# First ffn of an eight-phase model on one core: one product for router and latent, expert weights with the first stage, another pace of the sort

## The chip, the cores and the metric

The kernel runs on one core of one Trainium2 chip. The metric is the device time of one execution in microseconds (us), the median of the runs shown. All data are 32-bit floats unless a line says otherwise. The engines are named as in the profile: PE is TensorE's matrix product, PEld its weight load, DVE VectorE, ACT ScalarE, POOL GpSimd, SP SyncE, which here only issues DMAs.

## The reference

The input x is 8 batches of 256 tokens of 256 numbers. Eight sub-layers run one after the other, and after each comes x = layernorm(x + sublayer(x)): attention and feed-forward (ffn) in turn, four of each. The change touches the end of the first attention (attn0), the first ffn (ffn0), and in small ways the start of the second attention (attn1) and the last ffn's sort. attn0 is causal attention with 16 heads of 16 over 4 key heads. ffn0 is

```
scores = sigmoid(x @ gate.T)                  # 32 experts in 4 groups of 8
sb     = scores + gate_bias
groups = the 2 groups with the largest sum of their top two sb
chosen = top 8 of sb within the two groups
wts    = scores at chosen, over their sum, times 2.5
lat    = x @ fc1.T                            # 256 -> 128
routed = sum over chosen of wts_e * (relu(lat @ w1_e.T)**2 @ w2_e.T)
out    = routed @ fc2.T + relu(x @ shared_up.T)**2 @ shared_down.T
```

w1 and w2 are 32 matrices of 128 x 128 each, 2 MB each.

## The kernel before

The rows of x stay in SBUF for the whole kernel, as X[b] (tokens on partitions) and, transposed, as xT, four blocks of 512 tokens (two batches). A phase is a function; its weights are loaded on SP's queue by a `_load` function while the phase ahead runs, into a pool that lies at the other end of SBUF than the pool of the running phase. Working tiles of a phase are in a pool `act`, closed at its end. PSUM has four tags, "t", "a", "s" and "o", of two banks each. In attn0, ffn0, attn1, ffn2, attn3 and ffn3 the compute engines run in the order in which the code names the operations; work is interleaved by Python generators, where each `yield` hands over to another strand.

**attn0** (line 241). The loop over eight batches (480 to 512) runs, for batch b, the maxima of batch b+1, the exponentials of b, and between them `fill`, which takes one step of `finish` of an earlier batch, sometimes one step of a strand `ahead` (projections, at the end ffn0's shared expert on block 0), and two steps of the strand `sorting`. `finish` (386 to 439) makes the values, transposes them, multiplies by wo, adds and normalizes, and in its next step calls `norm_done(b)`, which transposes X[b] into xT (line 145). Behind batch 3 that step also starts the sort of ffn0's token group 0 (batches 0 to 3), so that it runs beside batches 4 to 7. `spread` (346) transposes HL, which POOL makes.

**The sort of a token group** (`ffn0_sort`, 947, with `place`, 840, `tile_experts`, 908, and `scatter`, 922). Each group has 8 tiles of 128 tokens. The sort computes the logits (962), sigmoid, the latents (977, copied twice by ACT, since each token goes to two expert groups), the two groups of each token, where each token's row comes to lie (counts and ranks, two products at 871), which expert group each tile belongs to (`r_te`, transposed at 917), and the weights of the eight experts. Then 16 indirect DMAs from POOL (928) write rows of 128 latents and 8 weights (544 bytes each) to a buffer `lrows` in DRAM, sorted by expert group.

**The experts** (`ffn0_experts`, 1071). Each token group gives 19 tiles of sorted rows, each of one expert group. SP fetches two tiles at a time as `xg` (1083). A tile is transposed (1099), multiplied by eight matrices of w1 (1107, two half steps), put through relu by ACT (1112) and squared by POOL (`hg`, 1114), multiplied by w2 (1124), and summed with its weights by DVE (1133, 1135); the sum goes to DRAM (`louts`, 1137). 19 tiles are 40 steps. `ffn0_combine` (1150 and on) gathers each token's two rows back, adds them, multiplies by fc2 and normalizes.

**ffn0** (1193) puts the strands in order: both expert weights are loaded into its `act` pool, each in four DMAs, on SP's queue behind attn1's weights (three of 2 MB). Then the shared expert on block 1 (`ffn0_shared`, 1042: four products up, each with relu and square, then two down), with the rest of attn0's strand and the first steps of group 1's sort; then group 0's 19 tiles beside group 1's sort; then the shared expert on blocks 2 and 3 beside `combine(0)`; then group 1's tiles beside the rest of it; `combine(1)` goes on into attn1.

**attn1** (1243) projects keys, queries and values per batch and group of heads (1273).

The shape of ffn0's order before is:

```
for i, _ in enumerate(self.ffn0_shared(w, 1, act)):
    if i == 1:
        for x in left:
            for _ in x:
                pass
    if i >= 2:
        next(sort, None)
    if i == 3:
        next(tiles)
for _ in tiles:
    next(sort, None)
```

Of the kernel before, what the change touches and what calls it, by code (L numbers as in the profile page):

```python
# [18 lines left out]
P = 128  # L19
# [20 lines left out]
class Model:  # L40
# [199 lines left out]

    def attn0(self, w, act, start=False, beside_then=None, between=()):

# [115 lines left out]
        def weights(b):  # L358

            qT, kT, o = qTs[b // 2], kTs[b // 2], (b % 2) * T  # L360
            for i, (kc, qc) in enumerate(((0, 0), (0, 1), (1, 1))):
# [15 lines left out]
                for s in range(4):  # L377
                    p = act.tile([P, 4, P], F32, tag=f"pT{i}{s}", name="pT")
                    nc.scalar.activation(p.rearrange("p h q -> p (h q)"), ps[s], AF.Exp)
                    if kc == qc:  # L380
                        nc.gpsimd.affine_select(
                            p, p, pattern=[[0, 4], [1, P]], compare_op=ALU.is_ge, fill=0.0,
                            base=0, channel_multiplier=-1,
                        )
                    pT[b, i, s] = p
                yield

        def finish(b):
# [48 lines left out]
            yield  # L437
            self.norm_done(b)
            if beside_then and b == GROUPS0[0][1] - 1:
                sorting.append(beside_then(act))  # L440
            yield

# [13 lines left out]

        ends, ahead, sorting, calls = [], [], [], [0]

# [6 lines left out]
        def fill(every=2):  # L465
            step(ends)
            calls[0] += 1
            if calls[0] % every == 0:
                step(ahead)
            for _ in range(2):  # L470
                step(sorting)

        def drain():
            while ahead:
                step(ahead)

        for _ in project(0):
            pass
# [3 lines left out]
        for b in range(NB):  # L482
            nxt = None
            if b == 0 or b % 2 == 1:
                drain()
                if (b + 3) // 2 < NBLK:
                    ahead.append(project((b + 3) // 2))
            if b + 1 < NB:
                nxt = maxima(b + 1)
            else:  # L490
                ahead.append(between)
            next(prev, None)
            mine = weights(b)
            for i in range(3):
                if nxt is not None:
                    next(nxt)
                fill(2 if b else 1)
                if i == 0:
                    spread(b)
                next(mine)  # L500
                fill(2 if 0 < b < NB - 1 else 1)
            if b == NB - 1:
                while ends:
                    step(ends)
            ends.append(finish(b))
            prev = nxt

        for _ in range(5):
            fill(1)
        while ahead or sorting:  # L510
            fill(1)
        return ends

# [331 lines left out]
    def place(self, w, act, keep, name, idx, n, E=32, tag="t"):  # L845
# [17 lines left out]
        )  # L863
        yield

        count, rank = (
# [41 lines left out]
    def tile_experts(self, w, act, keep, name, ends, tag="t"):  # L908

        nc, E = self.nc, ends.shape[1]  # L910
        past = act.tile([P, E], F32, tag="r_past", name="r_past", bufs=1)
        nc.vector.tensor_scalar(past, ends, w["iota"][:, 32:33], None, ALU.is_le)
        te = act.tile([P, 1], F32, tag="r_te", name="r_te", bufs=1)
        nc.vector.tensor_reduce(te, past, AX.X, ALU.add)
        nc.vector.tensor_scalar(te, te, float(E - 1), None, ALU.min)
        pt = self.ps(tag)[0:1, :P]
        nc.tensor.transpose(pt, te, self.ident)
# [19 lines left out]
    def ffn0_load(self, pool, keep):  # L937
        return dict(
            gate=self.load(pool, "f0_gate", [P, 2, 32]),
            bias=self.load_row(pool, "f0_bias", 32),  # L940
            fc1=self.load(pool, "f0_fc1", [P, 2, P]),
            behind=self.load(pool, "c_behind", [P, P]),
# [6 lines left out]
    def ffn0_sort(self, w, g, act, keep, tag="a"):  # L949
# [8 lines left out]

        lg = self.ps(tag)[:, : n * 32].rearrange("p (t e) -> p t e", e=32)
        for t in range(n):  # L960
            for c in range(2):
                nc.tensor.matmul(
                    lg[:, t, :], x(t, c), w["gate"][:, c, :], start=(c == 0), stop=(c == 1)
                )
        sc = act.tile([P, n, 32], F32, tag="r_sc", name="r_sc", bufs=1)
        nc.scalar.activation(sc, lg, AF.Sigmoid)
        sb = act.tile([P, n, 32], F32, tag="r_sb", name="r_sb", bufs=1)
        nc.vector.tensor_tensor(
            sb, sc, w["bias"].unsqueeze(1).to_broadcast([P, n, 32]), ALU.add
        )  # L970
        yield
        lat = keep.tile([P, n, 2, ROW0], F32, tag="lat", name="lat", bufs=1)
        for i in range(0, n, 4):
            pl = self.ps(tag).rearrange("p (t l) -> p t l", t=4)
            for t in range(4):
                for c in range(2):
                    nc.tensor.matmul(
                        pl[:, t, :], x(i + t, c), w["fc1"][:, c, :], start=(c == 0), stop=(c == 1)
                    )
            for k in range(2):  # L980
                nc.scalar.copy(lat[:, i : i + 4, k, 0:P], pl)
            yield

# [27 lines left out]
        )  # L1011
        expert = self.tile_experts(w, act, keep, f"f0{g}", ends, tag=tag)
        yield
# [25 lines left out]
        self.sorted0[g] = slots, expert  # L1039
        yield from self.scatter(self.lrows[g], slots, lambda t, k: lat[:, t, k, :])  # L1040

# [150 lines left out]

    def ffn0(self, w, act, keep, left, start=False):

# [3 lines left out]

        w1, w2 = (
            self.load(act, x, [P, 32, P], split=4).rearrange("p (g e) f -> p g (e f)", g=4)  # L1200
            for x in ("f0_w1", "f0_w2")
        )
        if 0 not in self.sorted0:
            if start:
                for b in range(NB):
                    self.transpose_x(b)
            for _ in self.ffn0_sort(w, 0, act, keep):
                pass
            for _ in self.ffn0_shared(w, 0, act):
                pass  # L1210
        sort = self.ffn0_sort(w, 1, act, keep)
        tiles = self.ffn0_experts(w1, w2, 0, act)
        for i, _ in enumerate(self.ffn0_shared(w, 1, act)):
            if i == 1:
                for x in left:
                    for _ in x:
                        pass
            if i >= 2:
                next(sort, None)
            if i == 3:  # L1220
                next(tiles)
        for _ in tiles:
# [4 lines left out]
        tiles = self.ffn0_experts(w1, w2, 1, act)  # L1227
        for blk in range(2, 4):
            for i, _ in enumerate(self.ffn0_shared(w, blk, act)):
                next(put, None)  # L1230
                if blk == 3 and i == 3:
                    next(tiles)
        for _ in tiles:
# [12 lines left out]
    def attn1(self, w, act, beside, then, start=False):  # L1246
# [6 lines left out]
        w["wo"] = self.load(act, "a1_wo", [P, 16, D], split=2)  # L1253
        gqk = act.tile([P, 1], F32, tag="gqk", name="gqk", bufs=1)
        nc.vector.tensor_tensor(gqk, w["gq"], w["gk"], ALU.mult)
        attTs, ends = {}, []

        class Unit:
# [5 lines left out]
            def begin(u):  # L1264
                u.qT = act.tile([P, 4, T], F32, tag="qT", name="qT")
                u.kT = act.tile([P, 4, T], F32, tag="kT", name="kT")
                u.rq = self.small.tile([P, 8], F32, tag="rq", name="rq")
                u.ssq = self.small.tile([P, 8], F32, tag="ssq", name="ssq")

            def project(u, which, t):  # L1270
                ps = self.ps("a")
                for c in range(2):
# [11 lines left out]
            def keys(u, t):  # L1284
                ps = u.kps[t] = u.project("wk", t)
                ssk = self.small.tile([P, 4], F32, tag="ssk", name="ssk")
# [28 lines left out]
            def turned(u, x, t):  # L1315
# [3 lines left out]
                tok = slice(t * P, (t + 1) * P)  # L1319
                if x is u.q:  # L1320
                    nc.vector.tensor_copy(u.qT[:, :, tok], pt)
                else:
                    nc.scalar.mul(u.kT[:, :, tok], pt, gqk)
# [537 lines left out]
    def ffn3_sort(self, w, g, act):  # L1861
# [33 lines left out]
        next(rows)  # L1895
        expert = self.tile_experts(w, act, self.const, f"f3{g}", ends)

# [157 lines left out]
def tile_layers(ctx: ExitStack, tc: tile.TileContext, ins, out, phases):  # L2055
# [6 lines left out]
    def open_weights(i):  # L2062
# [3 lines left out]
        if phases[i] in ("ffn0", "attn3"):  # L2066
# [3 lines left out]
            )  # L2070
            args = [kept[i]]
        pool = s.enter_context(tc.tile_pool(name=f"w{i}", bufs=1, side=sides[i % 2]))
        stack[i] = (s, load(pool, *args))
# [3 lines left out]
    for i, name in enumerate(phases):  # L2077
        m.last = i == len(phases) - 1
        with tc.tile_pool(name=f"act{i}", bufs=2, side=sides[i % 2]) as act:
# [3 lines left out]
            with tc.manual_schedule(engines=COMPUTE) if name in MANUAL else ExitStack():  # L2083
                if name == "attn0":
                    beside = None
                    if not m.last:
                        beside = partial(m.ffn0_sort, stack[i + 1][1], 0, keep=kept[i + 1])
                    between = iter(())
                    if not m.last:
                        between = m.ffn0_shared(stack[i + 1][1], 0, act, ("qT", "kh0"), bufs=3)  # L2090
                    left = m.attn0(w, act, start, beside, between)
                elif name == "ffn0":
                    left = m.ffn0(w, act, kept[i], left, start=start)
                elif name == "attn1":
# [19 lines left out]
def lay_out(i):  # L2114
# [24 lines left out]
    o["a0_wo"] = tiles(L0["attn_wo"])  # L2139
    o["f0_gate"] = tiles(L0["ffn_gate_w"].T)  # L2140
    o["f0_bias"] = L0["ffn_gate_bias"][None]
    o["f0_fc1"] = tiles(L0["ffn_fc1_w"].T)
    o["f0_fc2"] = L0["ffn_fc2_w"].T
# [94 lines left out]
```

## Time and profile before

| | |
|---|---|
| Median of 3 runs | 2625.83 us (2614.57 to 2627.1) |
| Profiled execution | 2678.61 us, its span 2676.9 us, mean granted TensorE clock 0.923 |
| Data moved by DMA in the span | 120.75 MB, 45 GB/s on average |
| Stretch of attn0 and ffn0 | from the start to about 580 us |
| First product of an expert | 361.30 us |
| Last steps of group 0's tiles | about 460 us |

The profile page shows one execution, in the span of which every instruction has a start and an end. Its second part cuts the span into 40 slices of 67 us and gives each engine's busy share in tenths, with the clock that TensorE was granted (`PEclk`, in tenths of full speed). A list of waits gives, for one engine, the instruction that stood idle (line and destination), what ended the wait, and the total, number and longest of such waits in us. A timeline row gives start, duration, engine, line, operation and operands, and in brackets the idle time before it with its releaser; on SP's queue a row is the issue of DMAs, and "x8" stands for eight of them. A table of windows gives, for a stretch, its length, the busy time (and number of instructions) of PE, PEld, DVE, ACT and POOL, the granted clock, the busy share of the 16 DMA engines and GB/s. A 32-bit product counts as several matmul records.

### The profile page before, as it was taken

The numbers are of one execution on the slowest core, as the hardware profiler recorded it, in microseconds if no ns is written. First come the engines' busy times: TensorE is split into PE (matmuls) and PEld (weight loads), VectorE is DVE, ScalarE is ACT, GpSimd is POOL, SyncE is SP. The second block draws the span as 40 slices with busy tenths as digits, with TensorE's granted clock in tenths as the row PEclk, the third lists the DMA queues.
The fourth block names the chain that finished last, engine by engine and source line by source line (L and its number), as shares of the span: only waits on it lengthen the run. The fifth ranks groups of instructions, "written<-read, shape, count | busy, mean of one in ns | idle before, by whom it ended". The sixth has DMA issues, their size and how long they took to land. (4 is left out here: it accounts for less than half of the span.)

```text
span 2676.9 us, 36134 instructions
## 1 busy us (share of the span) xinstructions
PE 2261.8 (84%) x12024; PEld 1535.6 (57%) x12080; DVE 1455.2 (54%) x3645; ACT 1020.2 (38%) x2911; POOL 934.1 (35%) x1637
## 2 busy tenths in 40 slices
PE   8997768989999999999999999997877777676780
PEld 4454457765666666666664465555555544465570
DVE  3546347665454444445455444556988887442353
ACT  1222224335454444445432112222767656433340
POOL 1221326444343333233312321001666648422315
PEclk9987879999999999999999999999989987687895
DMA  4000221110000100000070011002000001334553
GB/s 119 1 1 4 108 80 52 28 51 4 4 5 3 49 1 1 1 1 1 9 253 1 0 48 48 1 0 96 1 1 1 1 7 42 105 128 136 158 158 96
DMA packets 92451, 120.75 MB, mean 45 GB/s; under 512 B 9901, under 2 KB 79726, under 8 KB 91246
## 3 DMA queue, kind: packets, MB, share of 16 engines
q1 hardware_dynamic: 82846, 96.15, 11.1%
q0 software_dynamic: 8192, 21.11, 2.5%
q8 instruction: 101, 1.65, 0.2%
q10 hardware_dynamic: 1232, 1.18, 0.1%
q14 instruction: 80, 0.66, 0.1%
HBM read 67.53 MB, written 50.88 MB: 44 GB/s over the span
## 5 line engine op out<-in xcount | busy, mean ns | idle before, releaser
L1359 POOL TENSOR_SCALAR p<-p,rs 128x128 f32<-128x128 f32 (+1 forms) x256 | 104.2, 424 | 292.2 <-DVE rs L1357 281.2
L1349 ACT ACTIVATE p<-ps_s,nm,rq 128x128 f32<-128x128 f32 (+1 forms) x256 | 127.9, 506 | 147.4 <-DVE nm L1347 147.4
L137 POOL TENSOR_SCALAR rsq<-bnmv 128x2 f32<-128x2 f32 x64 | 13.9, 217 | 478.0 <-DVE bnmv L175 470.5
L1281 ACT ACTIVATE sq<-ps_a 128x512 f32<-128x512 f32 x128 | 77.0, 603 | 239.1 <-PE ps_a L1273 232.4
L1942 PE MATMUL ps_a<-w_f_gup,xTg 128*128 x504 | 119.2, 364 | 34.2 <-issue 22.4
L641 ACT ACTIVATE e<-ps_a,nm 128x128 f32<-128x128 f32 (+1 forms) x256 | 105.8, 435 | 102.7 <-DVE nm L638 94.5
L683 POOL TENSOR_SCALAR v<-e,r,nmd 128x128 f32<-128x128 f32 (+1 forms) x256 | 136.6, 544 | 10.1
L1273 PE MATMUL ps_a<-w_a_wq,xT 128*128 128x512 f32 x256 | 125.2, 612 | 15.8 <-DVE k L1293 12.9
L1282 DVE TENSOR_REDUCE ssk<-sq 128x4 f32<-128x512 f32 x64 | 43.8, 686 | 172.4 <-ACT sq L1281 172.4
L700 PE MATMUL ps_t<-ident,v 128*128 128x128 f32 x384 | 68.4, 316 | 63.6 <-DVE qT L579 29.1
L1273 PE MATMUL ps_a<-w_a_wv,xT 128*128 128x512 f32 x256 | 120.4, 593 | 0.0
L1273 PE MATMUL ps_a<-w_a_wk,xT 128*128 128x512 f32 x256 | 120.3, 593 | 0.0
L675 DVE SCALAR_TENSOR_TENSOR e<-e,c 128x128 f32<-128x128 f32 (+1 forms) x256 | 105.0, 460 | 27.2 <-POOL c L662 27.1
L1282 DVE TENSOR_REDUCE ssq<-sq 128x4 f32<-128x512 f32 x64 | 43.9, 686 | 132.8 <-ACT sq L1281 132.8
L1942 PEld LDWEIGHTS ps_a<-w_f_gup,xTg 128*128 128x128 f32 x504 | 88.5, 210 | 45.7 <-issue 28.1
L1114 POOL TENSOR_TENSOR hg<-rl 128x512 f32<-128x512 f32 x76 | 79.2, 1045 | 101.3 <-ACT rl L1112 100.6
L1397 PE MATMUL ps_o<-w_a_wo,attT 128*128 128x256 f32 x512 | 111.8, 379 | 0.0
L641 ACT ACTIVATE e<-ps_s,nm 128x128 f32<-128x128 f32 (+1 forms) x256 | 106.8, 453 | 0.0
L1135 DVE SCALAR_TENSOR_TENSOR yg<-ps_t,xg,yg 128x128 f32<-128x128 f32 x266 | 93.2, 350 | 24.5 <-PE ps_t L1124 15.8
L1397 PEld LDWEIGHTS ps_o<-w_a_wo,attT 128*128 128x128 f32 x512 | 96.7, 190 | 12.8
L145 PE MATMUL ps_t<-ident,X 128*128 128x128 f32 x256 | 49.3, 318 | 62.9 <-DVE X L181 53.1
L2003 POOL DMA_INDIRECT yk<-outs,r_slots x64 | 62.1, 970 | 111.5 <-DMA outs<-yg 60.6
(399 smaller groups left out, 6192.1 us busy)
## 6 DMA issues: line engine op xcount, KB each, us to landing
rows<-zero SPq DMA_DIRECT2D x42, 384.0 KB, 4.7
xg<-rows SPq DMA_DIRECT2D x42, 384.0 KB, 3.8
outs<-yg SPq DMA_DIRECT2D x42, 384.0 KB, 3.9
w_f_gup<-in_f_gup SPq DMA_DIRECT2D x8, 768.0 KB, 7.2
w_f_w<-in_f_w SPq DMA_DIRECT2D x8, 512.0 KB, 11.6
w_f_down<-in_f_down SPq DMA_DIRECT2D x8, 384.0 KB, 6.6
w_f_up<-in_f_up SPq DMA_DIRECT2D x5, 512.0 KB
lrows<-zero SPq DMA_DIRECT2D x12, 204.0 KB, 6.1
```

The costliest lines, as they stand in the source:

```text
L641: nc.scalar.activation(e[:, s, j * nk : (j + 1) * nk], sc[s][:, j, :], AF.Exp, bias=nm[:, s, j : j + 1], scale=1.0, accum_out=sums[:, s, j ...
L675: nc.vector.scalar_tensor_tensor(d[:, s, h, :], u.e[:, s, h, 1, :], u.c[:, s, h : h + 1], d[:, s, h, :], ALU.mult, ALU.add,)
L683: nc.gpsimd.tensor_scalar(u.v[:, s, h, :], d[:, s, h, :], u.r[:, s, h, 0:1], nm[:, s, h : h + 1], ALU.mult, ALU.add,)
L1114: nc.gpsimd.tensor_tensor(h[s], relu, relu, ALU.mult)
L1135: nc.vector.scalar_tensor_tensor(acc[j], y, c, acc[j], ALU.mult, ALU.add)
L1273: nc.tensor.matmul(ps, self.xt(u.b, t, c), w[which][:, c, u.cols], start=(c == 0), stop=(c == 1),)
L1281: nc.scalar.activation(sq.rearrange("p h d -> p (h d)"), ps, AF.Square)
L1282: nc.vector.tensor_reduce(out, sq, AX.X, ALU.add)
L1349: nc.scalar.activation(u.p[qc][:, h0 + j, :], sc[:, j, :], AF.Exp, bias=nm[:, j : j + 1], scale=r[:, j : j + 1], accum_out=u.sums[qc][:, h ...
L1359: nc.gpsimd.tensor_scalar(u.p[qc][:, j, :], u.p[qc][:, j, :], ri[:, j : j + 1], 1.0, ALU.mult, ALU.mult,)
L1397: nc.tensor.matmul(y[:, t, :], attTs[b][:, h, t * P : (t + 1) * P], w["wo"][:, h, :], start=(h == 0), stop=(h == 15),)
L1942: nc.tensor.matmul(ps, xT[j][:, c, :], w["gup"][:, bass.ds(er[j], 1), c, :].rearrange("p o f -> p (o f)"), start=(c == 0), stop=(c == 1),)
```

## The change

Seven edits, all of the order or place of work, but for the first:

1. gate and fc1 are one weight of 160 columns, `gate_fc1`; the sort makes logits and latents in one product, three tiles of tokens to a PSUM bank. DVE copies the logits out, ACT the latents to both places at once.
2. w1 is loaded by `ffn0_load`, hence on SP's queue at the start of attn0; w2 stays with ffn0. To make room, attn0's pool of exponentials `pT` goes from 24 buffers to 16, and the sort's tiles go to a pool of their own, `temp`.
3. In attn0 `norm_done(b)` leaves `finish` and is called in the first round of batch b+2; for batch 6 behind the loop, for batch 7 in ffn0, after two products of the shared expert on block 1.
4. The sort of group 0 starts at batch 6, takes one step a round in place of two, and what is left goes to ffn0: two steps for each step of the shared expert on blocks 1 and 2, finished before that of block 2 ends.
5. `place` and `tile_experts` have more yields, and the scatter yields after two DMAs. Both are used by ffn3's sort too.
6. The shared expert on block 2 comes before the tiles of group 0, group 1's sort runs wholly beside those tiles, and `combine(0)` runs beside block 3 alone.
7. In attn1, gqk moves to another pool, the first keys use PSUM tag "s", and qT is taken when first written.

```diff
-                    p = act.tile([P, 4, P], F32, tag=f"pT{i}{s}", name="pT")
+                    p = act.tile([P, 4, P], F32, tag="pT", name="pT", bufs=16)
...
-            self.norm_done(b)
-            if beside_then and b == GROUPS0[0][1] - 1:
-                sorting.append(beside_then(act))
-            yield
...
-            for _ in range(2):
-                step(sorting)
+            step(sorting)
...
+            if b == NB - 2 and beside:
+                sorting.append(beside)
...
+                if b > 1 and i == 0:
+                    self.norm_done(b - 2)
...
-            if b == NB - 1:
-                while ends:
-                    step(ends)
             ends.append(finish(b))
             prev = nxt
+        self.norm_done(NB - 2)
...
-        while ahead or sorting:
+        while ahead:
             fill(1)
...
-            gate=self.load(pool, "f0_gate", [P, 2, 32]),
+            gate_fc1=self.load(pool, "f0_gate_fc1", [P, 2, 32 + P]),
             bias=self.load_row(pool, "f0_bias", 32),
-            fc1=self.load(pool, "f0_fc1", [P, 2, P]),
+            w1=self.load(pool, "f0_w1", [P, 32, P], split=4),
...
+        for i in range(0, n, 3):
+            m = min(3, n - i)
+            ps = self.ps(tag)[:, : m * (32 + P)].rearrange("p (t l) -> p t l", t=m)
+            for t in range(m):
+                for c in range(2):
+                    nc.tensor.matmul(
+                        ps[:, t, :], x(i + t, c), w["gate_fc1"][:, c, :],
+                        start=(c == 0), stop=(c == 1),
+                    )
+            nc.vector.tensor_copy(lg[:, i : i + m, :], ps[:, :, 0:32])
+            nc.scalar.copy(
+                lat[:, i : i + m, :, 0:P],
+                ps[:, :, 32:].unsqueeze(2).to_broadcast([P, m, 2, P]),
+            )
+            yield
...
-        yield from self.scatter(self.lrows[g], slots, lambda t, k: lat[:, t, k, :])
+        rows = self.scatter(self.lrows[g], slots, lambda t, k: lat[:, t, k, :])
+        for i, _ in enumerate(rows):
+            if i % 2 == 1:
+                yield
...
+        w2 = self.load(act, "f0_w2", [P, 32, P], split=4)
+        w1, w2 = (x.rearrange("p (g e) f -> p g (e f)", g=4) for x in (w["w1"], w2))
...
+        for blk in (1, 2):
+            for i, _ in enumerate(self.ffn0_shared(w, blk, act)):
+                next(sort, None)
+                next(sort, None)
+                if blk == 1 and i == 1 and not start:
+                    self.norm_done(NB - 1)
+                if blk == 2 and i == 3:
+                    for _ in sort:
+                        pass
+                if blk == 2 and i == 4:
+                    next(tiles)
+        sort = self.ffn0_sort(w, 1, temp, keep)
         for _ in tiles:
             next(sort, None)
...
-        for blk in range(2, 4):
-            for i, _ in enumerate(self.ffn0_shared(w, blk, act)):
-                next(put, None)
-                if blk == 3 and i == 3:
-                    next(tiles)
+        for i, _ in enumerate(self.ffn0_shared(w, 3, act)):
+            next(put, None)
+            if i == 3:
+                next(tiles)
...
-                ps = u.kps[t] = u.project("wk", t)
+
+                first = u.b == 0 and u.g == 0
+                ps = u.kps[t] = u.project("wk", t, "s" if first else "a")
```

## The prediction

> **What bounds the kernel now.** I read the whole page first, for its engine shares and slices, then what TensorE waits for in the stretch that the change touches, then the timeline and the sums by stage there. All lines are of the profiled execution before.
>
> ```profile
> PE 2261.8 (84%) x12024; PEld 1535.6 (57%) x12080; DVE 1455.2 (54%) x3645; ACT 1020.2 (38%) x2911; POOL 934.1 (35%) x1637
> ...
> PE   8997768989999999999999999997877777676780
> ...
> PEclk9987879999999999999999999999989987687895
> ...
> PE 24%; DVE 12%; POOL 6%; issue 4%; ACT 2%; DMA 1%; another core or an unknown queue 0%; POOLq 0%; SPq 0%; DVEq 0%; ACTq 0%
> ```
>
> TensorE is the bound (84% busy, most of the chain), and the change takes almost no work from it. So the room is where its slice is below 9 or its clock below 9: slices 1 to 7 of 67 us each, which hold attn0's end and ffn0. TensorE's waits in 0 to 560 us say what is missing (line, who ended the wait, us in total, times, longest):
>
> ```profile
> PE ps_t L145 <- DVE X L181: 23.2, 16, 2.9
> PE ps_a L1099 <- DMA w_f_w<-in_f_w: 16.5, 1, 16.5
> PE ps_a L917 <- DVE r_te L915: 8.8, 2, 4.7
> PE ps_a L871 <- DVE r_one L858: 7.0, 2, 4.0
> ...
> PE ps_a L373 <- DVE E L350: 6.2, 6, 3.1
> PE ps_tb L346 <- POOL HL L340: 5.8, 1, 5.8
> ```
>
> Each is a transpose or product that stands in program order too soon behind what feeds it. Sums by stage (span, busy us of five engines, granted clock, DMA share):
>
> ```profile
> 200.00:361.00 161.00, 114.93 (x656) 67.10 (x657) 67.56 (x222) 35.52 (x63) 36.37 (x54) 0.82 0.20 76
> 361.00:460.00 99.00, 82.03 (x635) 76.95 (x634) 76.20 (x296) 41.41 (x56) 56.32 (x56) 0.93 0.13 35
> ```
>
> From 200 to 361 us TensorE is idle 46 us, and at clock 0.82 some 114.9 x 0.18 = 20.7 us of its busy time are lost. From 361 (first expert product) to 460 (last tile of group 0) VectorE is nearly as busy as TensorE. TensorE's timeline shows the one large hole:
>
> ```profile
> 331.48 1.95 PE L977 MATMUL ps_a<-w_f_fc,xT 128*128 128x128 f32 x16
> 349.91 0.45 PE L1099 MATMUL ps_a<-ident,xg 128*128 128x128 f32 x1 [16.48 <-DMA w_f_w<-in_f_w]
> 350.15 6.07 PE L1063 MATMUL ps_o<-w_f_down,hs 128*128 128x256 f32 x16
> ...
> 361.30 1.05 PE L1107 MATMUL ps_s<-xTg,wc 128*128 128x128 f32 x8
> ```
>
> and SyncE's shows why: all of attn1's weights and both expert weights are issued in a row, with the first token fetch behind them.
>
> ```profile
> 317.82 0.82 SPq L123 DMA_DIRECT2D w_a_wq<-in_a_wq  x2
> ...
> 323.06 16.74 SPq L123 DMA_DIRECT2D w_f_w<-in_f_w  x8
> 340.43 4.13 SPq L1083 DMA_DIRECT2D xg<-lrows  x4
> ```
>
> 10.5 MB from 317.8 to 349.9 us is 327 GB/s: the queue is full, and the tiles wait for it. The second row after the hole runs 6.07 us where the same 16 products take 3.62 at 357.84: the clock fell in the hole.
>
> **The change part by part.** R is attn0's last output product: 317.7 us before.
>
> *X transposes two batches later (norm_done).* Before 200 us X is waited for 9.7 us (7 times) and clock 0.83 in 140 to 200 costs 54.5 x 0.17 = 9 us, most of it at 185 to 195, full busy at clock 0.50. The transposes move behind a batch of other work, about 20 us of TensorE, so the 9.7 go; of the clock I take half. **-14.** What is late next: the output copies, covered by the same work. The eight fewer pT buffers are reused only after the value products of one half batch earlier: hidden by program order, and 0.6 us of ACT's wait each if not.
>
> *Sort later, one step a round, extra yields (200 us to R).* TensorE's idle before R is 10.0 (X), 5.8 (HL), 4.1 (r_te), 4.0 (r_one), 3.1 (E), 1.7 (r_upto): 28.7 us. HL is late because POOL stands in scatters; the scatter leaves attn0. r_te and r_one get a round between. I keep 7: **-22**. Clock here, 91.3 us busy at 0.84, loses 14.6; with the holes gone I keep 6: **-8**.
>
> Here the Trainium skill's rule is weighed ("TensorE: Matmul & The Clock Gate", Part 1: The HAM clock gate): the clock is half or full, falls after about one idle window of 3.4 us, and comes back after as long busy. The row first: 0.50 for about 10 us at full busy at 185 to 195, where no wait above 2.3 us is listed before 200 besides the loads at the start; and 14.6 us lost from 200 to R. By the rule only the waits over 3.4 us (HL, r_te, r_one) count, each 3.4 us at half clock or 1.7 lost: 5 us, so the two clock terms would be -4 instead of -12. The trace has short waits costing more than that, so I go by it, and let the rule's -8 smaller gain into the range.
>
> *One product for router and latent.* Gate is 32 matmuls in 3.86 us, fc1 2 x 1.95; merged, 32 of 160 columns, by the 0.122 us of 128 columns about 0.14 each: 4.5 us. **-3** for group 0 before R; group 1's goes from before the first tile into the tiles. The logits' extra copy (three on VectorE of about 0.3) hides beside shared work; one broadcast copy on ACT replaces two.
>
> *R to first expert product.* Before: 43.5 us (16.5 idle). After, 14 sort steps remain at R, two a step of shared(1): latent rows ready about R+15; the 16 scatters at 1.28 us spacing (POOL, 284.9 to 291.3) end at R+35.5; landing and fetch, 3.8 us by the page's issue part, R+40. The loads, SP's queue now 8.4 MB (w1 has gone in with attn0's start, where DMA is idle), end at R+26, so scatter takes the loads' place. TensorE has shared(1) 14.6, shared(2)'s ups 7.2 and half its down 3.6, with about 8 us of stalls on X of batch 7 and hs: it comes to the fetched rows at R+33, waits 7, and with the other half of down starts at **R+44.6: +1**. But shared(2), 14.6 us (459.8 to 474 before), is done in it: **-14.6** later.
>
> *Scatter in pairs, group 1's sort wholly beside tiles.* 361 to 460 was 15 sort steps in 52 us, 16 scatter steps of 2.25 us (scatter 1.2, POOL's hg 1.05) in 36, and 10 more. After: 24 sort steps, VectorE-bound (1.6 us of tile work each, about 20 of sort, 5 for the product and waits: 63), 8 of two scatters (3.45 each: 28), 8 plain (15): 106 against 99. **+7.** From the other side: at 4.5 us a pair, nothing overlapping, +15.
>
> *combine(0) beside six fewer shared steps:* its VectorE work is 20 us over 44 steps, so 6 more beside tiles at 0.46: **+3**. *attn1:* keys to another PSUM tag and qT taken late lift most of the 4.7 us wait at its start: **-3.5**. *ffn3:* the yields help r_te (5.7 us), but rounds there also stall for issue: between 0 and -6, **-2**.
>
> Sum: -14 -22 -8 -3 +1 -14.6 +7 +3 -3.5 -2 = **-56**. On the profiled 2678.6 us that is about 2622; that execution is 2% above the median of the runs, so on 2625.8 I forecast **2570**, -56 as it stands (in proportion it would be -55).
>
> **The rivals.**
> - *A, the scatter takes the loads' place and more* (the change doesn't do what it says: w1 was hidden by other late work). SP's 8.4 MB fill the 16 DMA engines from R to R+26 (share 0.90 at 318 to 350), and nine of the sixteen scatters run in that time; if each takes double, 9 x 1.28 = +11.5, and pairs at 4.5 us give +8. -56 + 20 = -36: **2590**. The skill speaks for it ("DMA: Bandwidth & Descriptors", SWDGE vs HWDGE): GpSimd writes its descriptors into SBUF, from which VectorE can lock it out in one of its modes, and the sort and tiles are VectorE's. Against: the 32 scatters traced last 0.96 to 1.24 us, with VectorE busy 27.3 of 37 us in 413 to 450. By the row scatters stay at 1.28 us, R+40; by the rule, if doubled throughout, R+60.
> - *Better:* the clock stays full throughout (20.7 + 9 lost: 17 more than I took) and the first rows are in time (7): **2546**.
> - *B, slower: each scatter stops the tiles.* In ffn3, from 2400 to 2420 us, 17 POOL instructions, mostly scatters, leave TensorE busy 4.6 us at clock 0.50: 0.9 us lost a scatter. Those 29 rows are 1 KB, here 544 bytes, and before's own scatters cost the tiles under 1.3. If each of the 32 now stops everything for the old 2.25 us step, +72 - 56: **2642**. It decides from 56/32 = 1.75 us a scatter, twice the row.
>
> **How the numbers follow.** Forecast 0.55 (2550 to 2592), A 0.27 (to 2612), better 0.13 (2530 to 2550), B 0.05. The range 2543 to 2610 leaves out half of the better case, the worst of A, and B: under 2 in 10. A measurement of this kernel tells about 0.5% from no change, so faster is below 2612.7, slower above 2639. Faster: all of forecast and better, most of A, 0.87; same 0.08, slower 0.05.
>
> **What would show it.** X waits at the transposes of attn0 gone; HL, r_te, r_one under 2 us; clock above 0.9 from 200 to 330; no wait for w1; a wait of about 7 us at the first xg; the tile phase of group 0 at 106 us; 15 us less from its end to the second's start. I am wrong if that xg wait is over 12 us, a pair of scatters over 4 us, or the clock in attn0 is still 0.84.

## The result, and the profile after

| | before | after |
|---|---|---|
| Median of the runs shown together | 2620.20 us (4 runs) | 2578.04 us (4 runs, 2576.09 to 2582.73) |
| Ratio to before | | 0.9841, 95% interval 0.9806 to 0.9875 |
| Profiled span | 2676.9 us, again 2625.5 us | 2580.8 us, again 2578.5 us |

The change takes 42 us off, by a second set of runs 44. The forecast was 2570 us, 56 off.

The first profile of before is no fair partner for the profile after. The same kernel profiled once more (first run below) has the same stages within 2 us up to the end of the third ffn and is 51 us shorter (attn3 5 us longer, the last ffn 58 shorter). All comparisons by stage below use this second profile of before.

The page of the kernel after, engines' shares and slices of 65 us:

```profile
PE 2234.2 (87%) x12016; PEld 1518.6 (59%) x12016; DVE 1454.7 (56%) x3651; ACT 1019.0 (39%) x2909; POOL 935.0 (36%) x1637
...
PE   8998788889999999999999999998878777668890
...
PEclk9998899999999999999999999999989988789995
```

TensorE is busy 34 us less than in the second profile of before (2268.5 us), with nearly the same matmuls. Most of that is a better clock: by the mean clocks of the two profiles (0.929 and 0.942) an estimate gives 2268.5 x 0.071 - 2234.2 x 0.058 = 31 us. By slice the clock is 8 or 9 in the slices 2 to 6, where it fell to 7 before. What TensorE waits for from 0 to 540 us (line, releaser, us in total, times, longest):

```profile
PE ps_t L145 <- DVE X L181: 10.3, 11, 2.2
PE ps_t L1128 <- POOL hg L1118: 8.4, 6, 1.5
PE ps_a L1103 <- DMA xg<-lrows: 5.9, 1, 5.9
...
PE ps_o L1067 <- DVE hs L1060: 4.5, 2, 3.8
...
PE ps_o L431 <- DVE aT L110: 3.6, 2, 2.2
...
PE ps_a L918 <- DVE r_te L914: 0.9, 1, 0.9
...
PE ps_tb L346 <- POOL HL L340: 0.6, 1, 0.6
```

Up to the first tile, X is waited for 4.1 us of those 10.3; the rest comes later, in ffn0. The wait for w1 (16.5 us, and 10.1 in the second profile of before) is gone, those for HL and r_te are under 1 us, and r_one is no longer in the list. One has grown among the tiles, from 1.0 to 8.4 us: the wait for POOL's `hg`, behind pairs of scatters. The sums by stage after (length, busy us of PE, PEld, DVE, ACT, POOL, clock, DMA share, GB/s), cut at attn0's last product (275), the first expert product (319), the end of group 0's tiles (424), group 1's first expert product (438) and the end of its tiles (538):

```profile
140.00:200.00 60.00, 58.23 (x414) 30.83 (x413) 36.70 (x68) 16.95 (x33) 17.44 (x33) 0.98 0.00 1
200.00:275.00 75.00, 64.75 (x352) 35.25 (x351) 37.89 (x144) 23.45 (x41) 12.34 (x24) 0.89 0.00 1
275.00:319.00 44.00, 31.71 (x100) 20.23 (x100) 17.75 (x63) 6.24 (x10) 18.16 (x18) 0.87 0.62 229
319.00:424.00 105.00, 84.14 (x662) 80.05 (x661) 76.55 (x299) 44.73 (x61) 55.74 (x56) 0.95 0.12 33
424.00:438.00 14.00, 13.99 (x51) 9.00 (x50) 5.67 (x12) 3.43 (x5) 4.00 (x4) 1.00 0.18 46
438.00:538.00 100.00, 88.01 (x671) 81.86 (x670) 74.60 (x210) 42.38 (x58) 55.09 (x58) 0.95 0.11 29
```

The rows before, up to its last product of attn0 at 318 us, are these (first profile; the second has the same clocks):

```profile
140.00:200.00 60.00, 54.48 (x298) 32.37 (x298) 26.85 (x51) 15.19 (x28) 11.24 (x21) 0.83 0.00 1
200.00:318.00 118.00, 91.29 (x546) 48.97 (x547) 61.33 (x209) 27.84 (x52) 35.12 (x52) 0.84 0.03 10
```

From 140 to 200 us the clock is 0.98 where it was 0.83. The third row after is the stretch that had the hole; TensorE's timeline there, and SP's queue:

```profile
289.12 7.57 PE L1067 MATMUL ps_o<-w_f_down,hs 128*128 128x256 f32 x26 [3.79 <-DVE hs L1060]
...
303.38 4.00 PE L1067 MATMUL ps_o<-w_f_down,hs 128*128 128x256 f32 x16
313.32 0.45 PE L1103 MATMUL ps_a<-ident,xg 128*128 128x128 f32 x1 [5.93 <-DMA xg<-lrows]
313.56 5.29 PE L1067 MATMUL ps_o<-w_f_down,hs 128*128 128x256 f32 x16
318.68 1.05 PE L1111 MATMUL ps_s<-xTg,wc 128*128 128x128 f32 x8
```

```profile
280.38 7.79 SPq L123 DMA_DIRECT2D w_f_w<-in_f_w  x4
310.99 1.91 SPq L1087 DMA_DIRECT2D xg<-lrows  x4
```

TensorE now does shared work in it, and what it waits for is the rows, fetched at 311 us, just after POOL's last scatter (308.56 to 309.52). The sixteen scatters begin at 287.68, when VectorE has made the first of the weights that they carry (287.37).

The stages of all kernels, from their profiles (us; R is the end of attn0's last output product; "tiles" from the first expert product of a group to its last). "attn3" is the time from the last normalization of the third ffn to that of attn3. Each kernel is explained below.

| kernel | R | R to first tile | tiles 0 | between | tiles 1 | attn3 |
|---|---|---|---|---|---|---|
| before, again | 318.2 | 43.8 | 98.3 | 29.3 | 93.6 | 514.6 |
| after | 274.7 | 44.0 | 105.5 | 14.1 | 100.0 | 520.9 |
| after, again | 273.3 | 44.8 | 104.5 | 14.1 | 98.7 | 521.9 |
| x_early | 298.1 | 43.5 | 105.9 | 14.1 | 99.0 | 522.4 |
| w1_late | 271.1 | 43.7 | 105.9 | 14.1 | 99.0 | 521.8 |
| sh2_late | 270.9 | 42.8 | 104.4 | 29.4 | 95.0 | 517.6 |
| sort_b5x2 | 296.1 | 31.8 | 106.6 | 14.1 | 97.5 | 519.0 |
| sort_b5 | 281.8 | 37.2 | 105.7 | 14.1 | 97.4 | 521.4 |
| split | 271.6 | 43.4 | 111.0 | 14.1 | 97.3 | 520.0 |
| single | 275.2 | 44.8 | 98.8 | 14.1 | 97.4 | 519.1 |
| no_yield | 280.7 | 42.7 | 107.6 | 14.1 | 98.9 | 514.2 |
| best1 | 273.0 | 44.9 | 97.8 | 14.1 | 98.3 | 514.1 |
| best2 | 273.9 | 42.2 | 92.6 | 14.1 | 99.7 | 515.5 |

### The profile page after: what moved, and what is told of

Its sections match the earlier page's. It is cut to its first block, busy times and chain, and to the rows that moved or that the text cites. A ratio compares the mean times of both kernels' runs of the same rounds, so it can differ in the third digit from the quotient of the medians.

```text
span 2580.8 us, 36064 instructions
## 1 busy us (share of the span) xinstructions
PE 2234.2 (87%) x12016; PEld 1518.6 (59%) x12016; DVE 1454.7 (56%) x3651; ACT 1019.0 (39%) x2909; POOL 935.0 (36%) x1637
## 5 line engine op out<-in xcount | busy, mean ns | idle before, releaser
L1282 DVE TENSOR_REDUCE ssk<-sq 128x4 f32<-128x512 f32 x64 | 43.8, 686 | 174.5 <-ACT sq L1281 174.5
L1946 PE MATMUL ps_a<-w_f_gup,xTg 128*128 x504 | 111.7, 346 | 14.7 <-DVE xTg L1940 6.8
L1128 PE MATMUL ps_t<-w_f_w,hg 128*128 x608 | 87.2, 290 | 18.2 <-POOL hg L1118 8.4
L697 PEld LDWEIGHTS ps_t<-ident,v 128*128 128x128 f32 x384 | 50.5, 164 | 88.7 <-POOL nmd L677 44.9
L1340 PE MATMUL ps_s<-kT,qT 128*128 128x256 f32 (+1 forms) x512 | 100.1, 329 | 0.0
```

The source lines that it names most:

```text
L697: nc.tensor.transpose(ps[:, s, c, :], x, self.ident)
L1340: nc.tensor.matmul(sc[:, j, :], u.qT[:, h0 + j, qc * P : (qc + 1) * P], u.kT[:, h0 + j, 0:nk], start=(j == 0), stop=False,)
L1946: nc.tensor.matmul(ps, xT[j][:, c, :], w["gup"][:, bass.ds(er[j], 1), c, :].rearrange("p o f -> p (o f)"), start=(c == 0), stop=(c == 1),)
```

## The experiments

The theory to be tested: attn0's end gains by the order of X's transposes and of the sort, the wait for w1 gives way to one for the scatter, and the shared expert's block 2 is done in that wait. The rivals to tell apart were that the load of w1 itself was the gain, that the sort's move did it alone, and that the scatter costs more in its new place. The runs are in three sets, each with its own runs of before beside it; ratios are to those. The smaller parts of the change (16 buffers of `pT`, the move of gqk, attn1's first keys on another PSUM tag) had no run of their own.

**Before and after once more** (b_again, a_again; nothing edited).

> The kernel before, profiled once more. The first profile was 58 us longer than the median of its runs, and TensorE's waits ended by 'issue' in the last ffn were 45 us, against 1 us in the profile of the changed kernel. If these 45 us belong to that one execution, this profile is near 2620 to 2630 us, and the stages before the last ffn stand as they did within 2 us (attn0's last product at 317.7, first expert product at 361.3). If the kernel before always stalls there and the extra yields in the sort cured it, the profile shows over 40 us of 'issue' again and is near 2680 us.

> The changed kernel once more, as the yardstick for the runs beside it: 2578 us within 0.3%, attn0's last product at 274.7 us, first expert product at 318.7, end of group 0's tiles at 424 us, each within 2 us.

Before: 2627.26 us, span 2625.5. After: 2580.12 us, ratio 0.9828 (0.9808 to 0.9848). The longest waits of TensorE in the last ffn, in the first profile of before ("issue" is time in which the engine waited for nothing that the profile shows):

```profile
PE ps_s L1955 <- issue: 23.5, 7, 8.9
PE ps_a L1942 <- issue: 21.8, 13, 10.2
```

and in the second:

```profile
PE ps_a L1942 <- issue: 1.3, 3, 0.6
```

So the 45 us are not the kernel's own. In the second set of runs below (sh2_late, single, sort_b5, no_yield), before has a median of 2685.21 us, all seven of its runs are over 2675, and the profiles of the four kernels beside it show 23 to 37 us of such waits in the last ffn: their whole times can be compared by ratio alone, and by stages ahead of it. The record lists the three sets on three chips (0, 8 and 4; the first profile's is not on record), so these waits may go with the chip as well as with the execution; no run tells the two apart. Gains of a few us are below the intervals of these ratios and are read from the stages.

**X's transposes at once again** (x_early).

```diff
             self.normed(b, r, *self.moments(r))
             yield
+            if b < NB - 1:
+                self.norm_done(b)
+            yield
...
-                if b > 1 and i == 0:
-                    self.norm_done(b - 2)
...
-        self.norm_done(NB - 2)
```

> Changed kernel with the X transposes of batches 0 to 6 back in finish, one step behind the normalization. If the moved transposes are what brought 14 us before 200 us and 10 of the 22 after it, attn0's last product comes 18 to 26 us later (X waits of some 20 us again, clock about 0.85 in 140 to 200 us) and the whole is 2597 to 2604 us. Rival: those waits were mostly made by the sort and the scatter in the same batches; then waits come back only in part and it is under 8 us later.

2601.44 us, ratio 0.9906 (0.9884 to 0.9928); R 23 to 25 us later, every stage behind it within 1.5 us of the changed kernel's. Its wait (100 to 420 us) and its clock from 140 to 200:

```profile
PE ps_t L145 <- DVE X L181: 17.0, 11, 2.5
```

```profile
140.00:200.00 60.00, 54.02 (x344) 27.88 (x344) 32.36 (x58) 12.83 (x25) 11.28 (x21) 0.91 0.00 1
```

The rival (the sort made those waits) falls: the sort still stands where the change put it, and half of the whole gain is gone. The clock from 140 to 200 us fell less than expected, to 0.91 and not to 0.85; what made the rest of the 0.83 before, no run shows.

**w1 loaded in ffn0 again** (w1_late).

```diff
-            w1=self.load(pool, "f0_w1", [P, 32, P], split=4),
...
-        w2 = self.load(act, "f0_w2", [P, 32, P], split=4)
-        w1, w2 = (x.rearrange("p (g e) f -> p g (e f)", g=4) for x in (w["w1"], w2))
+        w1, w2 = (
+            self.load(act, x, [P, 32, P], split=4).rearrange("p (g e) f -> p g (e f)", g=4)
+            for x in ("f0_w1", "f0_w2")
+        )
```

> Changed kernel with w1 loaded in ffn0 again, in front of w2 on SP's queue. By the diff's look the hole of 16.5 us was the wait for these 10.5 MB, so it should cost 8 to 16 us between attn0's last product and the first expert product. By my sum of that stretch the scatter has taken the loads' place: the loads end about 32 us after attn0's last product and the scatter's rows arrive at 39, so it costs 0 to 4 us.

2578.56 us, ratio 0.9825 (0.9803 to 0.9848): no loss at all. SP's queue and TensorE's first tile:

```profile
276.50 15.28 SPq L123 DMA_DIRECT2D w_f_w<-in_f_w  x8
307.33 1.91 SPq L1086 DMA_DIRECT2D xg<-lrows  x4
```

```profile
309.77 0.45 PE L1102 MATMUL ps_a<-ident,xg 128*128 128x128 f32 x1 [6.06 <-DMA xg<-lrows]
```

Eight loads stand in the queue instead of four, and the fetch still comes 36.2 us behind R (307.3 - 271.1), as in the changed kernel (311.0 - 274.7 = 36.3). The scatter ends last in both. The largest single wait in the first profile of before, 16.5 us, was named after this load, and moving the load is worth nothing once the sort stands where it does. The two profiles of before say the same of the wait's size: 16.5 and 10.1 us, with the first tile 43.6 and 43.8 us behind R.

**The shared expert's block 2 behind the tiles again** (sh2_late).

```diff
-        for blk in (1, 2):
-            for i, _ in enumerate(self.ffn0_shared(w, blk, act)):
...
+        for i, _ in enumerate(self.ffn0_shared(w, 1, act)):
+            next(sort, None)
+            next(sort, None)
+            if i == 1 and not start:
+                self.norm_done(NB - 1)
+            if i == 4:
+                for _ in sort:
+                    pass
+                next(tiles)
...
-        for i, _ in enumerate(self.ffn0_shared(w, 3, act)):
+        for blk in range(2, 4):
+            for i, _ in enumerate(self.ffn0_shared(w, blk, act)):
```

> Changed kernel with the shared expert on block 2 behind group 0's tiles again (beside combine(0)), the sort of group 0 finished beside block 1. If that work only fills a wait for the scatter, the wait at the first xg grows from 6 to about 20 us, the first expert product stays 40 to 45 us behind attn0's last product, and the 14.6 us come back after the tiles, with 2 to 4 us of clock lost in the hole: 2594 to 2600 us. Rival: the shared expert's own ACT and VectorE work holds up the sort beside it, so without it the scatter starts earlier, the first product comes by 34 us, and the whole is below 2588 us.

```profile
307.92 0.48 PE L1103 MATMUL ps_a<-ident,xg 128*128 128x128 f32 x1 [18.59 <-DMA xg<-lrows]
```

The wait is 18.6 us, and the first product comes 42.8 us behind R, about as in the changed kernel: the work filled a wait, and the scatter, not the shared expert, sets the tile's start. The 15.3 us come back between the tiles. But the ratio is 0.9855 (0.9828 to 0.9883), little over the changed kernel's. Tiles 1 takes 4 to 5 us less, since `combine(0)` has six more shared steps to run beside, and attn1 ends 2 us sooner behind the tiles. So from R to the end of attn1 block 2's move is worth 6 to 8 us, not 15.

**Sort earlier: one step a round, and two** (sort_b5, sort_b5x2; the second line only in sort_b5x2).

```diff
-            if b == NB - 2 and beside:
+            if b == NB - 3 and beside:
...
-            step(sorting)
+            for _ in range(2):
+                step(sorting)
```

> Changed kernel with group 0's sort started one batch earlier (batch 5), still one step a round: its steps are done by attn0's end and the scatter starts there. If the scatter sets the first expert product (my sum), the wait of 6 us at xg goes, and that of 4.5 us for hs with it: 34 to 38 us in place of 44 from attn0's last product to the first expert product, attn0 0 to 3 us longer: 2571 to 2576. Rival: the sort beside more of attn0 costs there what it saves behind (VectorE and POOL late for HL and X): attn0 6 or more us longer, the whole 2578 to 2584.

> Changed kernel with group 0's sort and scatter back in attn0: from batch 5, two steps a round as before. If the later sort is what saved the waits for HL, r_te and r_one (my 22 us less the 10 for X, and part of the clock), attn0's last product comes 12 to 20 us later than in the changed kernel, but the rows are in DRAM by then and the first expert product follows after about 29 us instead of 44: the whole 2575 to 2585, that is, moving the sort gave nearly nothing by itself. If attn0 loses less than 8 us, it is 2568 to 2573 and the later sort was a loss.

sort_b5: ratio 0.9818 (0.9789 to 0.9846); R 7 to 8 us later, the first tile 7 us nearer to it: one for one, as the rival had it. sort_b5x2: 2582.89 us, ratio 0.987 (0.9854 to 0.9887); R 21 to 23 us later and the first tile 12 to 13 us nearer. Its waits from 190 to 430 us bring back what the profile of before had, but for r_te's:

```profile
PE ps_t L145 <- DVE X L181: 8.8, 4, 3.2
...
PE ps_a L870 <- DVE r_one L856: 6.9, 1, 6.9
PE ps_tb L346 <- POOL HL L340: 6.1, 1, 6.1
PE ps_a L373 <- DVE E L350: 2.9, 1, 2.9
```

So the later sort saves 22 us in attn0 and spends 12 to 13 of them behind it; some 8 to 11 us up to the end of tiles 1 are its own gain, and 3 to 5 of the span (2583.8 against 2580.8 and 2578.5). The clock goes with the two moves in turn: in this run it is 0.99 from 140 to 200 us and 0.81 from there to R, in x_early 0.91 and 0.90, in the changed kernel 0.98 and 0.89.

**Router and latent as two products** (split).

```diff
+        pg = self.ps(tag)[:, : n * 32].rearrange("p (t e) -> p t e", e=32)
+        for t in range(n):
+            for c in range(2):
+                nc.tensor.matmul(
+                    pg[:, t, :], x(t, c), w["gate_fc1"][:, c, 0:32],
+                    start=(c == 0), stop=(c == 1),
+                )
+        nc.vector.tensor_copy(lg, pg)
+        yield
```

and the latents from columns 32 on, four tiles to a bank, copied twice.

> Changed kernel with router and latent as two products again (same weight tile, sliced), the rest as changed. By the rows the merged product saves 3 us of TensorE per token group: attn0's last product 2 to 4 us later for group 0; for group 1 beside tiles, where VectorE is the limit, 0 to 3 us. Whole: 2580 to 2585. If the sort's pace is set by its steps and not by the products, no change within 1 us at either place.

2583.13 us, ratio 0.987 (0.9854 to 0.9887). R is not later (271.6), the tiles 0 stretch is: 111.0 against 104.5 to 105.5 us. The merged product is worth nothing in attn0 and 6 us beside the tiles, the other way round than I had it for this run. Beside the tiles TensorE is busy 90.1 us in it, against 85.6 in the changed kernel once more: so 4.5 of the 6 us are found in TensorE's own time. The run also puts the copies out of PSUM back into their old form, and the two were not told apart.

**One scatter a step** (single).

```diff
-        for i, _ in enumerate(rows):
-            if i % 2 == 1:
-                yield
+        for _ in rows:
+            yield
```

> Changed kernel with one scatter a step as before. By the step times, group 1's scatter takes 8 steps of 3.51 us in the changed kernel and leaves 8 plain ones of 1.85, 43 us together; one a step is 16 steps of 2.25, 36 us: group 0's tile stretch 105.5 -> 99 us, the whole about 2572. Rival: what does not overlap is POOL's own time for scatter and hg, which is the same, and the steps after are VectorE's: no change within 2 us.

Tiles 0 takes 98.8 us, 6 to 7 less; ratio 0.9804 (0.9776 to 0.9831). POOL in the changed kernel:

```profile
388.54 1.00 POOL L929 DMA_INDIRECT lrows<-lat,r_slots  x1 [0.17 <-issue]
389.85 0.97 POOL L929 DMA_INDIRECT lrows<-lat,r_slots  x1 [0.30 <-issue]
390.84 1.05 POOL L1118 TENSOR_TENSOR hg<-rl 128x512 f32<-128x512 f32 x1
392.05 1.00 POOL L929 DMA_INDIRECT lrows<-lat,r_slots  x1 [0.17 <-issue]
```

and with one scatter a step:

```profile
388.61 0.99 POOL L929 DMA_INDIRECT lrows<-lat,r_slots  x1 [0.17 <-DVE yg L1138]
389.63 1.05 POOL L1117 TENSOR_TENSOR hg<-rl 128x512 f32<-128x512 f32 x1
390.84 1.00 POOL L929 DMA_INDIRECT lrows<-lat,r_slots  x1 [0.17 <-issue]
```

A half tile comes every 3.51 us with pairs and every 2.23 with singles. POOL is the limit of these steps either way: from 384 to 412 us it is busy 23.3 us with pairs and 23.6 with singles. With singles twice as many tile steps lie beside its scatters (TensorE is busy 27.0 us there instead of 20.6), and fewer plain ones, without scatter or sort, are left over.

**Without the extra yields** (no_yield).

```diff
         )
         yield
-        yield

         count, rank = (
...
         nc.vector.tensor_scalar(te, te, float(E - 1), None, ALU.min)
-        yield
-        yield
```

> Changed kernel without the three extra yields in place and tile_experts (they act in both ffn0 sorts and in the last ffn's). In ffn0, r_one and r_te waits come back, about 4 us each and group: attn0's last product 5 to 8 us later, group 0's tiles 4 to 8 us longer. In attn3 and the last ffn, which are 5 us longer in the changed kernel than in the kernel before (785 against 780.6): if the yields cost that, it goes back to 780; if it is the order of something else, it stays at 785. Whole: 2585 to 2592 by the first, 2579 to 2585 if ffn0's waits are hidden.

Ratio 0.9828 (0.9798 to 0.9857): as the changed kernel, but made up of two that cancel. R is 6 to 7 us later and tiles 0 2 to 3 longer, with waits for r_te (5.4 us, 2 times) and r_one (3.5) back. attn3, beside which the last ffn's sort runs, is 514.2 us, as in before. Over all profiles attn3 is 517.6 to 522.4 with the yields in that sort (nine) and 509.6 to 515.5 without (five). It lies at the end of attn3: from the fourth-last normalization to the last are 156 to 160 us with them and 148 to 150 without.

**Two versions put together** (best1, best2). best1 is single, with the extra yields kept in ffn0's sorts alone:

```diff
-        yield
+        if name[:2] == "f0":
+            yield
```

(both yields of `tile_experts` likewise). best2 adds to it:

```diff
+        sort1 = self.ffn0_sort(w, 1, temp, keep)
...
                 if blk == 2 and i == 4:
+                    for _ in range(3):
+                        next(sort1)
                     next(tiles)
-        sort = self.ffn0_sort(w, 1, temp, keep)
+        sort = sort1
```

> Changed kernel with one scatter a step in ffn0 and without the extra yields in the last ffn's sort alone (ffn0's sorts keep them). If the two gains seen one by one are separate, group 0's tiles take 99 us and attn3 ends 514 us after the third ffn, 7 us sooner: 12 us under the changed kernel, ratio to the kernel before about 0.978. If the longer attn3 was not the yields' doing, only the 6 us of the tiles come, ratio about 0.981.

> As best1, and group 1's three products for router and latent stand before the first tile, where TensorE waits about 5 us for the rows. If that wait has room for them (4.5 us of TensorE), the first expert product comes at the same time and the tile stretch has three steps with sort work fewer: 2 to 4 us under best1. If the latents' copies, which must wait until group 0's scatter has read the same buffer, hold up the first tile, it is 0 to 3 us over best1.

best1: 2568.33 us, ratio 0.982 (0.9804 to 0.9836). By its stages both gains are there (97.8 and 514.1 us) and its span is 2563.1, but the ratio misses the 0.978 I expected and cannot be told from the changed kernel's, which was not run in this set. best2: **2557.64 us, ratio 0.9773** (0.9757 to 0.979), an interval clear of those of before and of the changed kernel. Its first tile:

```profile
307.63 4.66 PE L969 MATMUL ps_a<-w_f_gate_fc,xT 128*128 128x160 f32 x32
312.48 0.30 PE L1104 MATMUL ps_a<-ident,xg 128*128 128x128 f32 x1 [0.19 <-DMA xg<-lrows]
312.62 3.62 PE L1068 MATMUL ps_o<-w_f_down,hs 128*128 128x256 f32 x16
```

The three products fill the wait for the rows to 0.2 us, and the product after it, 5.29 us in the changed kernel, takes 3.62: the clock granted in it is 1.00, against 0.67. With three steps of sort fewer, tiles 0 takes 92.6 us. The fear that the latents' copies hold up the tile did not come true.

## Why the prediction was right, and where it was off

The time, 2578, lies in the range; the direction and the mechanism held. By its own terms, measured by the second profile of before against the two of after:

| step | forecast | measured | run that shows it |
|---|---|---|---|
| X later, before 200 us and to R | -24 (-14, and 10 of the 22) | -23 to -25 | x_early |
| sort later, yields, clock, to R | -20 (the rest of -22, and -8) | -21 to -23 | sort_b5x2 |
| merged product, group 0 | -3 | 0 | split |
| R in all | -47 | -44 to -45 | profiles |
| R to first tile | +1 | 0 to +1 | profiles |
| shared block 2 gone from between | -14.6 | -15.2 | sh2_late |
| tiles 0 | +7 | +6 to +7 | single |
| tiles 1 | +3 | +5 to +6 | sh2_late, for 4 to 5 |
| attn1 | -3.5 | -2 | profiles |
| second ffn to third ffn | 0 | -2 | profiles; cause open |
| last ffn's sort | -2 | +5 in attn3 and the last ffn | no_yield |

The shares up to R overlap somewhat: without the extra yields alone, R is 6 to 7 us later (no_yield).

By these rows the kernel gained 45 of the 56 us, and the eleven that are missing are mainly three terms. Seven are the last ffn's sort, where the sign was wrong: I took its yields for a gain because r_te waits 5.7 us there, and did not look at whom they make late. attn3, beside which it runs, is about 7 us shorter without them. No run isolates the wait that carries it, but the traces narrow it down to POOL, which makes attn3's `v` and issues the sort's scatters. With the yields TensorE's waits for `v` in attn3's second half come to 5.4 to 7.6 us in all nine profiles, without them to 0.2 to 1.3 in all five. The longest of them, in the changed kernel, has three scatters on POOL ahead of `v`, from 2263.96 us on:

```profile
2269.90 1.22 PE L697 MATMUL ps_t<-ident,v 128*128 128x128 f32 x4 [4.11 <-POOL v L680]
```

The last scatter comes 118 us behind the fourth-last normalization in both profiles of the changed kernel, and 97 to 98 us behind it in the five without the yields. Two to three are tiles 1: the price of 0.46 us a step was VectorE's busy time alone, and by sh2_late the six steps cost 0.6 to 0.8 us each. Three are the merged product in attn0, where R comes no sooner for it; why, no run shows. One and a half more are attn1, and the two that nobody forecast behind it make up for them by luck.

In tiles 0 the sum was right in its parts: a pair of scatters took 3.51 us where it had 3.45, and the 7 us that it gave for pairs (28 and 15 against 36) are what single gets back.

Of the rivals, A's price is refuted: the sixteen scatters took 0.95 to 1.42 us each, the wait at xg was 5.9 us and a pair 3.51, not 4.5. The loads are not what made some of them slower (last section). A's core, that w1 would have been hidden by other late work, is shown by w1_late, and was in the forecast's own sum of R to the first tile. B did not happen: no stage beside ffn0's scatters is longer by more than the 7 us of tiles 0. Of the two parts of the better case, one, the first rows in time, was to be had by order (best2).

The clock was rightly taken from the rows. By the Trainium skill's rule of idle windows of about 3.4 us ("TensorE: Matmul & The Clock Gate", Part 1: The HAM clock gate) I would have booked -4; 58.2 us busy at 0.98 instead of 54.5 at 0.83, and 64.8 at 0.89 instead of 91.3 at 0.84 (busy time times the clock's lack: 1 against 9, 7 against 15), make it about -15. In x_early, with no wait for X over 2.5 us, the clock in 140 to 200 is 0.91. What was off in the list of signs is the clock from 200 to 330: 0.87 to 0.89 up to the first tile, where I asked for 0.9.

## What to carry to other kernels

The longest wait in a profile names what came last, not what would be gained: before moving a load, work out when the next-late source arrives, here the scatter, and fill the wait with work that is to be done anyway, as best2 does. What a step is worth depends on the stage it lands in: the same merged product was worth nothing in attn0 and 6 us beside the tiles. A change to a helper that two phases share changes both phases: the extra yields helped ffn0 and cost 7 us in attn3, and best1 gives them to one caller only.

## What the runs showed of the hardware

The last ffn's stretch of "issue" waits, some 45 us in one profile, was there in one execution of the kernel before and not in another (spans 2676.9 and 2625.5 us), and in one set of runs before's median rose to 2685.21 us. What sets it stays open, the chip among the candidates.

TensorE's clock fell behind waits under 2.5 us. In the first profile of before the longest waits between 100 and 200 us are three of 2.3 us, for X. Behind the one that ends at 121 us the clock stayed 1.00, behind the one at 152 it fell to 0.79 for 5 us, and behind the third, below, it fell to 0.50 (third figure from the end), though TensorE is busy in all of the last two rows:

```profile
181.70 1.33 PE L145 MATMUL ps_t<-ident,X 128*128 128x128 f32 x4 [2.28 <-DVE X L181]
```

```profile
180.00:185.00 5.00, 3.30 (x7) 1.79 (x8) 1.35 (x2) 3.24 (x5) 3.70 (x8) 0.60 0.00 0
185.00:190.00 5.00, 5.00 (x21) 4.11 (x19) 0.69 (x1) 0.00 (x0) 0.00 (x0) 0.50 0.00 0
190.00:195.00 5.00, 5.00 (x25) 5.00 (x25) 0.43 (x1) 0.38 (x1) 0.00 (x0) 0.50 0.00 2
```

In the changed kernel no wait from 140 to 200 us is over 0.6 us, and the clock is 1.00 up to 195. So the length of a single wait does not tell what it costs here.

A queue with 2 MB less of loads gave nothing to 16 scatters of 544-byte rows. Their spacing was 1.27 us for most and 1.7 us for three of them, with eight loads ahead as with four. The slow ones go with VectorE: in the changed kernel the loads fill the DMA engines (share 0.95) up to 299 us, and the scatters behind the first keep their 1.27 us there; each of the slow ones, behind 299, starts just behind a square of the shared expert's block 2:

```profile
300.78 0.69 DVE L1060 TENSOR_TENSOR hs<-relu 128x512 f32<-128x512 f32 x1 [1.02 <-ACT relu L1059]
```

```profile
300.89 1.42 POOL L929 DMA_INDIRECT lrows<-lat,r_slots  x1 [0.30 <-issue]
```

In sh2_late, where block 2 is not beside them, all but the first take 0.96 or 0.97 us. By what way the square holds up the scatter, and whether it is the one that rival A named, no run shows.
